# Layer 0 of a four-layer graph kernel: features by twos, bf16 parts moved into the dense sums, loads on other queues

## The chip, the cores and the metric

One Trainium2 chip, one core used. The metric is device time of one execution in microseconds (us), the median over runs. Engines: PE is TensorE (PEld its weight loads), DVE is VectorE, ACT is ScalarE, POOL is GpSimd, SP is SyncE, which only issues transfers here. PEclk is the granted TensorE clock, 1.00 being full speed.

## The reference, cut to what matters

Four layers follow each other on a graph of 4096 nodes with 256 features. Only layer 0, a dense graph attention with 8 heads, is touched by the change:

```python
def _L0_gnn_ref(x, W, b, a, adj_matrix):              # N=4096, D=256, H=8
    node_feats = (x @ W.T + b).reshape(num_nodes, num_heads, half)
    logit_parent = (node_feats * a[None, :, :half]).sum(axis=-1)
    logit_child = (node_feats * a[None, :, half:]).sum(axis=-1)
    attn_logits = logit_parent[:, None, :] + logit_child[None, :, :]
    attn_logits = jax.nn.leaky_relu(attn_logits, 0.2)
    attn_logits = jnp.where(jnp.abs(adj_matrix)[..., None] != 0.0, attn_logits, 0.0)
    attn_probs = jax.nn.softmax(attn_logits, axis=1)
    out = jnp.einsum('ijh,jhc->ihc', attn_probs, node_feats)
    return out.reshape(num_nodes, -1)
# x = layernorm(x + _L0_gnn_ref(...)); three more layers with the same adjacency follow
```

## The kernel before: the parts that matter

Layer 0 has three steps. **Features**, in 32 blocks of 128 nodes: the node features, exponentials of the child logits, their split into a coarse and a fine part (`src`, hi and lo) for the dense sums, and into three bf16 parts (`gb`, stored to `gmd`) for the attention. **Dense sums**: for each of 16 pairs of blocks, the adjacency is loaded (`a`), cast to the matmul's format (`ar`), stored again for the later layers (`adjs`), turned into a bf16 mask (`nad`), and multiplied by `src` into `pz`: 4096 matmuls in 128 groups of 32, one group for each `ar`. **Attention**: in two halves of four heads, signs of logits are compared with the mask and multiplied by the bf16 parts.

```python
# attention: loads, all but `na` on ACT's queue
for half in range(2):
    for b in range(0, NB, 8):
        nc.scalar.dma_start(gm[:, b:b + 8], gmd[half, :, b:b + 8])
    for it in range(N // IT):
        for g in range(NB // K):
            nc.sync.dma_start(na[:, g * K:(g + 1) * K], nad[it, :, g * K:(g + 1) * K, :])
        for hh in range(H // 2):
            nc.scalar.dma_start(lpb, ...)             # parent logits of this head
            nc.scalar.dma_start(z, ...)
            # ... per group of 4 blocks: ACT sg = sign(lpb + lc), DVE gt = sg > na, PE acc += gt^T gm
# ...
# sums0: features, one block at a time, with everything of the block in the loop
work = tile_pool(name="l0aw", bufs=2)
ps   = tile_pool(name="l0aps", bufs=1, space=PSUM)
psz  = tile_pool(name="l0apz", bufs=3, space=PSUM)
for b in range(NB):
    # ... load x, 2 transposes, 2 matmuls -> pn, add the bias -> nf, lp, lc; ex = exp(lc), exp(0.2 lc)
    v = work.tile([P, H, 2, C1], F32, name="v")
    for s in range(2):
        nc.vector.tensor_mul(v[:, :, s, :], nf, ex[:, s]...)
    for i, t in ((0, v[:, :, 1, :]), (1, nf)):        # hi and lo parts for the dense sums
        nc.scalar.copy(hi, t)
        nc.vector.tensor_sub(lo, t, hi)
    gb = work.tile([P, H, 3, 2 * C1], BF16, name="gb")
    nc.scalar.copy(gb[:, :, 0, :], vv)                # three bf16 parts for the attention
    nc.vector.tensor_sub(vv, vv, gb[:, :, 0, :])
    nc.scalar.copy(gb[:, :, 1, :], vv)
    nc.gpsimd.tensor_sub(vv, vv, gb[:, :, 1, :])
    nc.gpsimd.tensor_copy(gb[:, :, 2, :], vv)
    for half in range(2):
        nc.scalar.dma_start(gmd[half, :, b], gb[...])
# ... total = sums of src over all nodes: 64 matmuls, one copy
# dense sums
for b in range(0, NB, 2):
    pz = [psz.tile([P, 2, 512], F32, name="pz") for _ in range(2)]
    for g in range(NB // 4):
        a = work.tile([P, 2, G, P], F32, name="a", bufs=2)
        for q in range(2):
            nc.sync.dma_start(a[:, q], self.adjt[b + q, :, g * G:(g + 1) * G, :])
        ar = work.tile([P, 2, G, P], F32R, name="ar")          # two buffers, from the pool
        nc.vector.tensor_copy(ar, a)
        nb = work.tile([P, G, 2, P], BF16, name="nb")
        for q in range(2):
            nc.scalar.activation(nb[:, :, q, :], a[:, q], AF.Copy, scale=-1.0, bias=1.0)
            nc.gpsimd.dma_start(self.adjs[b + q, ...], ar[:, q])
        nc.gpsimd.dma_start(nad[it, ...], nb)
        # ... 32 matmuls pz[q][:, t] += ar[:, q, k]^T src[:, jc, t, s]
    for q in range(2):
        # ... zt from pz on ACT and DVE, stored to zd
```

## Time and profile before

| | before |
|---|---|
| time, median of 4 runs (lowest to highest) | 5450.6 us (5443.5 to 5451.7) |
| features, until `total` is copied | 224.5 us |
| last dense matmul | 705.5 us |
| first attention matmul, last attention matmul | 734.5, 1710.9 us |
| layers 1 to 3 begin their first large product (`ps_sup`) | 1776.9 us |

The places in time are read from the timeline.

The timeline at the turn between the halves (start, duration, engine; in brackets the idle time before it and what ended it):

```profile
1211.16 0.33 ACTq L216 DMA_DIRECT2D gm<-gmd  x1
...
1216.67 0.59 ACTq L225 DMA_DIRECT2D lpb<-lpd  x1
...
1221.23 4.41 ACTq L225 DMA_DIRECT2D lpb<-lpd  x1
1228.21 8.42 ACT L242 ACTIVATE sg<-lpb,lc 128x1024 bf16<-128x1024 f32 x8 [25.10 <-DMA lpb<-lpd]
```

The last load of `gm` could only go at 1211.16, when half 0 had released its tile; the loads of `lpb` stand behind it in ACT's order, and ACT then waited 25.10 us for them.

### The profile page before, as it was taken

The numbers are of one execution on the slowest core, as the hardware profiler recorded it, in microseconds if no ns is written. First come the engines' busy times: TensorE is split into PE (matmuls) and PEld (weight loads), VectorE is DVE, ScalarE is ACT, GpSimd is POOL, SyncE is SP. The second block draws the span as 40 slices with busy tenths as digits, with TensorE's granted clock in tenths as the row PEclk, the third lists the DMA queues.
The fourth block names the chain that finished last, engine by engine and source line by source line (L and its number), as shares of the span: only waits on it lengthen the run. The fifth ranks groups of instructions, "written<-read, shape, count | busy, mean of one in ns | idle before, by whom it ended". The sixth has DMA issues, their size and how long they took to land. (4 is left out here: it accounts for less than half of the span.)

```text
span 5447.4 us, 72422 instructions
## 1 busy us (share of the span) xinstructions
PE 4418.2 (81%) x25835; PEld 3512.0 (64%) x25836; DVE 3488.5 (64%) x8177; ACT 2870.9 (53%) x5723; POOL 444.1 (8%) x807
## 2 busy tenths in 40 slices
PE   6899967767774899688888888886788888887799
PEld 4699967766774785466666566644555555555677
DVE  4322258887887222877776677619988888888322
ACT  4433369979994103655555555446555555555211
POOL 3344400000001210000000000000000000000000
PEclk6799989999997998799999999997999999999899
DMA  4599953342222593111122211241111111111466
GB/s 150 193 342 346 341 195 106 132 150 91 96 94 74 169 308 104 43 63 63 64 72 72 65 63 63 70 145 37 59 57 57 57 57 57 57 57 59 157 227 202
DMA packets 333884, 655.57 MB, mean 120 GB/s; under 512 B 73537, under 2 KB 146113, under 8 KB 324289
## 3 DMA queue, kind: packets, MB, share of 16 engines
q1 hardware_dynamic: 189824, 436.29, 24.1%
q10 hardware_dynamic: 112960, 113.79, 6.3%
q0 software_dynamic: 30720, 100.69, 4.8%
q8 instruction: 208, 3.41, 0.3%
q14 instruction: 172, 1.40, 0.1%
HBM read 490.46 MB, written 160.17 MB: 119 GB/s over the span
## 5 line engine op out<-in xcount | busy, mean ns | idle before, releaser
L1061 PE MATMUL ps_a<-X,aT 128*128 128x256 f32 x4096 | 1075.0, 421 | 469.5 <-ACT aT L1058 469.5
L1061 PEld LDWEIGHTS ps_a<-X,aT 128*128 128x128 f32 x4096 | 844.8, 212 | 691.2 <-ACT aT L1058 564.0
L249 PE MATMUL acc<-gm,gt 128*128 128x198 bf16 x8192 | 748.3, 250 | 253.0 <-DVE gt L244 241.5
L242 ACT ACTIVATE sg<-lpb,lc 128x1024 bf16<-128x1024 f32 x832 | 870.9, 1135 | 119.5 <-DVE gt L244 78.9
L249 PEld LDWEIGHTS <-gt 128*128 128x128 bf16 x8192 | 694.7, 98 | 306.5 <-DVE gt L244 283.7
L1058 ACT COPY aT<-ps_tp 128x512 f32<-128x512 f32 x512 | 278.9, 583 | 698.3 <-PE ps_tp L1056 698.1
L380 PE MATMUL pz<-src,ar 128*128 128x264 f32 x4096 | 549.7, 294 | 44.9 <-ACT src L337 33.0
L244 DVE TENSOR_TENSOR gt<-sg,na 128x4096 bf16<-128x4096 bf16 x208 | 474.1, 2286 | 164.6 <-ACT sg L242 164.6
L380 PEld LDWEIGHTS pz<-src,ar 128*128 128x128 f32 x4096 | 522.9, 194 | 66.2 <-ACT src L337 43.8
L138 PE MATMUL ps_r<-XD,adj_piece 128*128 128x512 f32 x2048 | 506.2, 399 | 13.0 <-DMA adj_piece<-adjs 7.3
L811 ACT ACTIVATE ja<-e,nc 128x2048 bf16<-128x2048 f32 x256 | 509.6, 1991 | 0.0
L138 PE MATMUL ps_adj<-XD,adj_piece 128*128 128x512 f32 x2048 | 494.9, 399 | 16.3 <-DMA adj_piece<-adjs 11.2
L138 PEld LDWEIGHTS ps_r<-XD,adj_piece 128*128 128x128 f32 x2048 | 376.8, 188 | 152.5 <-DMA adj_piece<-adjs 23.6
L138 PEld LDWEIGHTS ps_adj<-XD,adj_piece 128*128 128x128 f32 x2048 | 385.3, 190 | 100.5 <-DVE XD L113 11.9
L841 DVE SCALAR_TENSOR_TENSOR v<-e,c 128x4096 bf16<-128x4096 f32 x96 | 429.4, 4472 | 1.1
L947 DVE SCALAR_TENSOR_TENSOR e<-e,edge 128x256 f32<-128x256 f32 x1024 | 415.1, 479 | 2.0
L76 POOL TENSOR_SCALAR ln_var<-ln_mv 128x1 f32<-128x1 f32 (+1 forms) x144 | 35.3, 245 | 4522.9 <-DVE ln_mv L74 1680.1
L753 PE MATMUL ps_logit<-kT,q 64*128 64x512 f32 x1024 | 350.8, 654 | 47.6 <-ACT e L757 45.9
L901 DVE MAX8 cand<-v 128x8 f32<-128x256 f32 x1024 | 350.4, 412 | 4.0
L372 ACT ACTIVATE nb<-a 128x512 bf16<-128x512 f32 x256 | 158.2, 629 | 341.6 <-DMA a<-in_adjt_dram 254.7
L757 ACT ACTIVATE e<-ps_logit 128x1024 f32<-128x1024 f32 x256 | 261.8, 1030 | 114.0 <-PE ps_logit L753 110.7
L897 DVE SCALAR_TENSOR_TENSOR v<-e,hi 128x2048 f32<-128x2048 f32 x128 | 300.9, 2351 | 2.1
(281 smaller groups left out, 4798.0 us busy)
## 6 DMA issues: line engine op xcount, KB each, us to landing
adj_piece<-adjs SPq DMA_DIRECT2D x256, 512.0 KB, 5.4
adj_piece<-adjs SPq DMA_DIRECT2D x512, 256.0 KB, 3.5
a<-in_adjt_dram SPq DMA_DIRECT2D x256, 256.0 KB, 5.6
adjs<-ar POOLq DMA_DIRECT2D x256, 256.0 KB, 5.6
na<-nad SPq DMA_DIRECT2D x64, 1024.0 KB, 6.2
nad<-nb POOLq DMA_DIRECT2D x128, 256.0 KB, 5.1
lpb<-lpd ACTq DMA_DIRECT2D x32, 512.0 KB, 5.0
gmd<-gb ACTq DMA_DIRECT2D x64, 198.0 KB, 2.1
```

Source lines behind the costliest of these rows:

```text
L138: nc.tensor.matmul(ps, a[:, k, :], rhs(jc).rearrange("p s d -> p (s d)"), start=(jc == 0), stop=(jc == self.NB - 1))
L242: nc.scalar.activation(sg[:, k, :], lpb, AF.Sign, bias=lc[:, jc, h:h + 1])
L244: nc.vector.tensor_tensor(*flat, ALU.is_gt)
L249: nc.tensor.matmul(acc[:, q, :6 * C1], gt[:, k, q * P:(q + 1) * P], gm[:, jc, hh, :], start=(jc == 0 and q % 2 == 0), stop=(jc == NB - 1 a ...
L380: nc.tensor.matmul(pz[q][:, t, :W], ar[:, q, k, :], src[:, jc, t, s], start=(jc == 0 and s == 0), stop=(jc == NB - 1 and s == 1))
L753: nc.tensor.matmul(pl[:, s, :], q[s * A:(s + 1) * A, :], kT[s * A:(s + 1) * A, c * 512:(c + 1) * 512], start=True, stop=True)
L811: nc.scalar.activation(ja, e[:, s * HALF:(s + 1) * HALF], f, bias=nc1, accum_out=fs[:, i + s:i + s + 1])
L841: nc.vector.scalar_tensor_tensor(junk, e, c, e, op0=ALU.is_ge, op1=ALU.mult, accum_out=S)
L897: nc.vector.scalar_tensor_tensor(v, ec, hi, ec, op0=ALU.is_lt, op1=ALU.mult, accum_out=sb[:, s:s + 1])
L901: nc.vector.max(cand[:, 8 * j:8 * j + 8], v[:, k * 256:(k + 1) * 256])
L947: nc.vector.scalar_tensor_tensor(ec, ec, edge[:, j:j + 1], ec, op0=ALU.is_ge, op1=ALU.mult)
L1061: nc.tensor.matmul(pa[:, :D], aT[:, k * P:(k + 1) * P], X[:, jc, :], start=(jc == 0), stop=(jc == NB - 1))
```

## The change

Its intent: shorten the features (two blocks a step, PSUM buffers of their own, without the bf16 parts), make the bf16 parts beside the dense sums of the first pairs, let the dense sums have two pairs of `pz` buffers, and take the attention's loads off ACT's queue. The diff, cut to its core:

```diff
-            psz = ctx.enter_context(tc.tile_pool(name="l0apz", bufs=3, space=PSUM))
-            for b in range(NB):
-                x = work.tile([P, 1, D], F32, name="x", bufs=3)
+            for b in range(0, NB, 2):
+                x = work.tile([P, 2, D], F32, name="x", bufs=3)
+                px = ps.tile([P, 512], F32, name="ps_x", bufs=2)
+                pn = ps.tile([P, 2, 512], F32, name="ps_nf", bufs=2)
   ... (the same operations, two blocks wide; one subtraction moves from DVE to POOL)
+                for q in range(2):        # the sums for `total`, now inside the loop
+                    for k in range(2):
+                        nc.tensor.matmul(pt[:, :W], one, src[:, b + q, 1, k], ...)
-                gb = work.tile([P, H, 3, 2 * C1], BF16, name="gb")      # no longer here
-                ...
+            pre.close()                   # PSUM of the features is given back
+            nc.scalar.activation(elc, both[:, :, 1, :], AF.Exp)
+            psz = ctx.enter_context(tc.tile_pool(name="l0apz", bufs=4, space=PSUM))
+            def factored(b):
+                v = work.tile([P, H, 2, C1], F32, name="vf")
+                nc.vector.tensor_add(v[:, :, 1, :], part(0, 0), part(0, 1))   # hi + lo again
+                nc.vector.tensor_add(v[:, :, 0, :], part(1, 0), part(1, 1))
+                nc.vector.tensor_mul(v[:, :, 0, :], v[:, :, 0, :], elc[:, b]...)
+                gb = work.tile([P, H, 3, 2 * C1], BF16, name="gb")
+                nc.scalar.copy(gb[:, :, 0, :], v)
+                nc.vector.tensor_sub(v, v, gb[:, :, 0, :])
+                nc.scalar.copy(gb[:, :, 1, :], v)
+                nc.gpsimd.tensor_sub(v, v, gb[:, :, 1, :])
+                nc.gpsimd.tensor_copy(gb[:, :, 2, :], v)
+                for half in range(2):
+                    nc.scalar.dma_start(gmd[half, :, b], gb[...])
             for b in range(0, NB, 2):
                 pz = [psz.tile([P, 2, 512], F32, name="pz") for _ in range(2)]
+                for q in range(2):
+                    factored(b + q)
   ... attention
-                for b in range(0, NB, 8):
-                    nc.scalar.dma_start(gm[:, b:b + 8], gmd[half, :, b:b + 8])
                     for g in range(NB // K):
                         nc.sync.dma_start(na[...], nad[...])
+                        if it == 0:
+                            nc.sync.dma_start(gm[:, g * K:(g + 1) * K], gmd[half, :, g * K:(g + 1) * K])
-                        nc.scalar.dma_start(lpb, ...)
+                        nc.gpsimd.dma_start(lpb, ...)
-                        nc.scalar.dma_start(z, ...)
+                        nc.gpsimd.dma_start(z, ...)
```

## The prediction

> **What bounds the kernel now.** The change touches layer 0 only, so I cut the span there into stages at places read from the timeline: features 0 to 225 us (with the first pair of dense sums between them), dense sums to 706, first loads of the attention to 735, attention half 0 to 1211, the turn between the halves to 1235, half 1 to 1717, and the rest, in which order and forms of the instructions stay as they are. Stretches of the trace, with busy us of each engine, TensorE clock, DMA share, GB/s:
> ```profile
> core 0: us, PE busy (x) PEld busy (x) DVE busy (x) ACT busy (x) POOL busy (x), PEclk, DMA share, GB/s
> 0.00:225.00 225.00, 154.68 (x558) 109.13 (x560) 109.92 (x281) 103.54 (x314) 80.36 (x132) 0.70 0.42 140
> 225.00:706.00 481.00, 468.93 (x3828) 464.27 (x3826) 102.27 (x181) 153.23 (x266) 222.08 (x355) 1.00 0.96 340
> 706.00:735.00 29.00, 1.17 (x7) 0.85 (x8) 7.25 (x20) 8.24 (x9) 0.00 (x0) 0.57 0.85 346
> 735.00:1211.00 476.00, 373.04 (x4095) 346.62 (x4092) 410.57 (x334) 428.31 (x410) 0.00 (x0) 0.99 0.33 117
> 1211.00:1235.00 24.00, 0.27 (x4) 0.14 (x3) 7.15 (x10) 6.79 (x7) 0.00 (x0) 0.59 0.73 271
> 1235.00:1717.00 482.00, 374.46 (x4096) 347.48 (x4094) 415.15 (x343) 428.61 (x410) 0.00 (x0) 0.98 0.25 82
> ```
> In the features no engine is full, the clock is 0.70 and DMA idles more than half the time: a chain from engine to engine. In the dense sums PE is 97% busy at full clock and the DMA share is 0.96: two limits close together. Two stretches, 29 and 24 us, have hardly any PE work. The waits of the first 900 us say why:
> ```profile
> ACT nb L372 <- DMA a<-in_adjt_dram: 254.7, 159, 4.9
> DVE ar L369 <- DMA adjs<-ar: 192.1, 60, 5.7
> ...
> POOL v L345 <- ACT gb L344: 96.1, 32, 4.0
> ...
> DVE nf L317 <- PE ps_nf L314: 64.2, 32, 3.4
> ...
> ACT sg L242 <- DMA gm<-gmd: 15.1, 1, 15.1
> ```
> POOL and DVE wait on ACT and PE once in each of 32 feature blocks: one block's chain hardly overlaps the next. The dense sums wait for DMA on the feeding engines, not on PE: its matmuls waited for `ar` 1.1 us in all. The last line is the gap at 706; at the turn between the halves the same query shows
> ```profile
> PE acc L249 <- DVE gt L244: 94.7, 69, 23.7
> ...
> ACT sg L242 <- DMA lpb<-lpd: 25.1, 1, 25.1
> ```
> and the timeline shows the loads of `lpb` issued at 1216.67 and 1221.23 on ACT's queue, behind the four loads of `gm`, the last of which waited for the end of half 0 (the last matmul of it near 1211).
>
> **What the Trainium skill says.** (1) "TensorE: Matmul & The Clock Gate", section "Part 1: The HAM clock gate": the array runs at half clock unless it has been busy for about 3.4 us. The trace agrees: 0.70 in the features, 1.00 in the dense sums, 0.57 in the gaps. (2) "PSUM — Partial Sum Buffer", section "Specifications (TRN2)": eight banks of 2 KiB per partition. Four `pz` buffers of two banks are thus all of PSUM, and no dense sum can start before the features have closed theirs. The trace of before, with three `pz` buffers, does overlap them. (3) "DMA: Bandwidth & Descriptors", section "Issuing engines are not separate DMA queues": issuing from other engines only saves sequencer time, "usually small relative to the DMA itself". Here it was not small: the load behind `gm` held ACT 25.1 us. (4) "Perfetto Trace Analysis", section "Roofline": 358 GB/s is a core's share of HBM, one core alone can reach about 120% of it. Here the dense sums move 340 GB/s at a share of 0.96, and loads of `na` and `gm` alone some 410.
>
> **The change part by part.**
> *Features by twos.* Before, 32 blocks take about (225 - 12 - 8 for the 64 matmuls of `total`) = 205 us, 6.4 us each, and contain the 256 dense matmuls of pair 0. After, 16 steps of two blocks; nothing of the bf16 parts (ACT 2 x 0.63, DVE 0.71, POOL 1.12 + 0.68 us a block) and no `pz` matmul is in them. PE's work in a step, from pitches in the timeline at low clock (feature matmuls 0.50 us: four in 2.02; the rest estimated from their width): 4 transposes x 0.22 + 4 feature matmuls x 0.50 + 2 small transposes x 0.22 + 4 sums x 0.23 = 4.2 us; at full clock (four in 1.24) about 2.3. The order on PE takes two steps together: features of A and B, then sums of A, sums of B. The sums wait for the longest path, DVE add 0.8, ACT copy 0.63, POOL subtraction 1.12, each with a hop of about 0.1 us. Followed through two steps at low clock I get about 9.7 us, at full clock about 7; I take 8.5. So 8 x 8.5 = 68 us, plus 12 us of start, plus tail and `total`: about 84 us, in place of 225.
> *Dense sums.* PE now has all 4096 matmuls here. Its best pitch before is 85 in 10 us, 0.1176 us, its mean 481/3828 = 0.1257, with dips where one pair's `pz` is read; four buffers remove these. PE alone would need 4096 x 0.1176 = 482 us. But the bytes: `a` 67.1 + `adjs` 67.1 + `nad` 33.5 + `zd` 8.65 + `gmd` 12.7 = 189 MB, of which some 4 MB go early, since only two `a` and two `ar` buffers can fill during the features. At 340/0.96 = 354 GB/s when full, 185 MB take 523 us; at the mean rate of before, 544. I choose 532: DMA becomes the bound, PE has slack. The bf16 parts (per block DVE three adds or multiplications at about 0.45 and 0.71, ACT 1.26, POOL 1.8 us) come some eight per nine groups in the first four pairs, by the order of instructions. There POOL has 1.08 + 0.76 + 1.8 = 3.6 us per group of 32 matmuls, which PE could do in 3.8. So POOL also runs nearly full for the first 36 groups and may make them 5 us each: 36 x 5 + 92 x 3.9 = 539, close to the DMA figure and not to be added to it.
> Features and dense sums end at 84 + 532 = 616, against 706: **-90 us**. Most of what the features gain goes back, since before they carried about 31 MB, some 90 us worth of transfer, under their idle time.
> *First attention loads.* `sg` needs `lpb`, which now goes out on POOL's queue, not what stood behind `gm`. Its first record can come about when `fac` is done, near 713 instead of 727.8. Then four `sg` 4.3 us and `gt` 2.3 us bring the first matmul to about 721 instead of 734.5; `na` and `gm` come in turn, 1.84 MB per group or 4.5 us at 410 GB/s against 4.2 us for four `sg`, so about 1 us is lost again: **-12 us**.
> *The turn between the halves.* `gm` is loaded piece by piece behind `na` on SP as the last head releases it, `lpb` is on another queue and prefetched a head ahead: the 23.7 us wait of PE goes, **-24 us**. In the rest of the attention ACT and DVE are both at 86 to 90% and take turns; two fewer issues per head on ACT were hidden anyway: 0.
> Sum: -90 - 12 - 24 = -126, 5450 - 126 = **5324**.
>
> **Rivals.** (a) PE stays the bound of the dense sums, because the DMA share near 1 counts waiting packets and not capacity. For it: 10 us pieces at 377 GB/s occur; PE hardly waited for `ar`. Against: in twelve such pieces after 235 us the share was 0.90 to 1.01, and the mix is fixed. Then the stage takes about 500 us, the whole 5290. (b) The loop of two `ar` buffers gets longer: cast 0.7, hop, issue 1.1, landing 5.6 make 8.3 us for two groups, 4.15 each, already what PE's mean pace of 4.0 is. POOL is in order, so bf16 work that waits for ACT holds up the writes of `adjs`; with 5.5 us for 36 groups and 4.1 after it the stage takes 575, the whole 5367. The 192 us wait of DVE for `adjs` speaks for it. (c) Two steps do not overlap, since the sums that are now inside the loop wait for POOL: 8 us a step, 16 x 8 = 128 us, end at 144, the whole 5384. Against it: `px` and `pn` have two buffers each, and the work per step is half of before. (d) SWDGE descriptors for `lpb` are slow while DVE works, and the turn keeps a gap: plus 10 to 25 us. Prefetch by a head of 30 us speaks against.
>
> **Range and chances.** The dense stage gives -30 to +40 us, the features -10 to +40, the attention -5 to +15. These do not all go the same way; I take 5270 to 5380. The 2% line is 5341, only 17 us above the centre. I give 0.65 to faster by over 2%, 0.34 to within 2%, 0.01 to slower.
>
> **What would show it right or wrong.** Features: last sum of `total` before about 95 us, clock there not under 0.65, no `pz` matmul earlier. Dense sums: 500 to 560 us long, DMA share at or above 0.97 and near 350 GB/s, PE with visible waits on `ar` in place of waits on `pz`; first four pairs slower than the rest. Attention: no ACT wait on `lpb` or `gm` over 5 us, first matmul about 14 us after the last dense sum, no gap of PE at the turn. After the attention every stage equal to within 5 us. Wrong it is if the dense stage runs at PE's pitch (sum too small), or over 570 us, or if POOL's in-order queue holds PE for more than 30 us in all.

## More of the kernel before

From the page, the span in 40 slices of 136 us (layer 0 is the first thirteen), then the group of the dense matmuls (busy us, mean ns, idle time before them):

```profile
PE   6899967767774899688888888886788888887799
...
PEclk6799989999997998799999999997999999999899
DMA  4599953342222593111122211241111111111466
...
L380 PE MATMUL pz<-src,ar 128*128 128x264 f32 x4096 | 549.7, 294 | 44.9 <-ACT src L337 33.0
```

The first slice and a half are the features: in the first slice PE is at 6, the clock at 6 and DMA at 4. Slices 3 to 5 are the dense sums, where PE and DMA are both near 9. The dense matmuls' idle time is due to `src`, that is to pair 0, which ran inside the features.

## The result, and the profile after

The changed kernel takes 5366.6 us (5364.5 to 5370.0, 4 runs) against 5450.6 us. The ratio is 0.9849, interval 0.9832 to 0.9866: 1.5% faster, and within the 2% band. Ratios and intervals here are from runs of both kernels in the same rounds; they are close to the ratio of the medians quoted, but not quite the same.

The page after, the same rows as above:

```profile
PE   7799977777774997888888888877788888887799
...
PEclk9999999999997997999999999988999999999899
DMA  5899952232223780111112222141111111111466
...
L402 PE MATMUL pz<-src,ar 128*128 128x264 f32 x4096 | 521.3, 289 | 51.7 <-DVE ar L391 51.0
```

The clock is 0.9 from the first slice, and the dense matmuls now wait for `ar` (51.0 us) where they had waited for `src`. In the second slice PE stands at 7 only, though all of it lies in the dense sums. The stretches of time after, cut at its own stages (length, busy us of each engine with its instructions, clock, DMA share, GB/s):

```profile
0.00:88.00 88.00, 58.37 (x289) 43.86 (x290) 46.67 (x105) 41.32 (x94) 28.94 (x47) 0.98 0.34 105
88.00:300.00 212.00, 171.17 (x1277) 167.10 (x1278) 94.97 (x176) 83.05 (x145) 129.01 (x178) 0.92 0.87 303
300.00:660.00 360.00, 349.62 (x2820) 345.22 (x2820) 75.36 (x133) 113.59 (x197) 164.08 (x263) 1.00 0.95 337
660.00:678.00 18.00, 1.67 (x9) 1.04 (x8) 7.77 (x20) 10.04 (x11) 2.89 (x4) 0.56 0.77 271
678.00:1155.00 477.00, 371.83 (x4058) 344.03 (x4057) 407.19 (x333) 431.70 (x413) 24.43 (x33) 0.98 0.35 126
1155.00:1634.00 479.00, 375.86 (x4136) 348.82 (x4133) 418.44 (x347) 430.44 (x412) 25.35 (x34) 0.99 0.27 96
```

The features end at 88 us, at a clock of 0.98. The dense sums take two stretches. In the first, 212 us long, the bf16 parts are made: 1277 matmuls are 39.9 groups of 32, so 5.3 us a group. In the second, 2820 matmuls in 360 us are 88 groups of 4.09 us. The gap before the attention has shrunk from 29 to 18 us, and the row of 24 us at the turn between the halves has gone: the halves meet at 1155 and each lasts as long as before. Stage by stage, from the timeline:

| us | before | after | difference | predicted |
|---|---|---|---|---|
| features, until `total` | 224.5 | 87.4 | | 84 |
| last dense matmul | 705.5 | 660.0 | -45.5 | -90 |
| from there to the first attention matmul | 29.0 | 17.6 | -11.4 | -12 |
| attention, first to last matmul | 976.4 | 956.3 | -20.1 | -24 |
| from there to `ps_sup` | 66.0 | 65.8 | -0.2 | 0 |
| all after it | | | -7.5 | 0 |
| span of the profiled execution | 5447.4 | 5362.7 | -84.7 | -126 |

So the features came as predicted, and so did the two gaps. What is missing is in the dense sums: from 87.8 to 660.0 they took 572 us, not 532. The -7.5 us after `ps_sup` lie in layers whose instructions are the same. They are no more than the scatter of the kernel before over chips (5443.5 to 5456.4 us), and nothing here explains them.

The chain of waits of the kernel after in its first 900 us (engine and tile, what it waited for, total us, times, longest):

```profile
ACT nb L394 <- DMA a<-in_adjt_dram: 233.5, 136, 5.3
...
DVE ar L391 <- DMA adjs<-ar: 134.6, 46, 7.6
...
PE pz L402 <- DVE ar L391: 51.0, 33, 8.6
...
ACT gb L372 <- DMA gmd<-gb: 39.0, 15, 5.8
```

DVE waits 134.6 us for `adjs` stores to release one of the two `ar` buffers, almost all of it (119.9 us) after 300 us. ACT waits for stores of `gmd` to release one of the two `gb` buffers, all of it before 300 us. PE waits for `ar` 40.8 us of its 51.0 between 90 and 290 us. What such a moment looks like in the timeline:

```profile
181.69 0.71 DVE L373 TENSOR_TENSOR vf<-vf,gb 128x528 f32<-128x528 f32 x1 [3.25 <-ACT gb L372]
186.99 0.63 ACT L372 CAST gb<-vf 128x528 bf16<-128x528 f32 x1 [5.33 <-DMA gmd<-gb]
...
187.65 0.71 DVE L373 TENSOR_TENSOR vf<-vf,gb 128x528 f32<-128x528 f32 x1 [5.25 <-ACT gb L372]
...
188.28 1.62 DVE L391 CAST ar<-a 128x1024 fp32r<-128x1024 f32 x1
...
189.95 1.47 PE L402 MATMUL pz<-src,ar 128*128 128x264 f32 x5 [7.28 <-DVE ar L391]
```

ACT stands 5.33 us for a `gmd` store to land. DVE's subtraction stands behind ACT, the cast of `ar` stands behind the subtraction in DVE's order, and PE idles 7.28 us for want of `ar`. What the clock does meanwhile, by the microsecond (busy us of PE, PEld, DVE, ACT and POOL with their instructions, then clock, DMA share, GB/s):

```profile
186.00:187.00 1.00, 0.00 (x0) 0.00 (x0) 0.00 (x0) 0.01 (x1) 0.00 (x0) 1.00 0.17 65
188.00:189.00 1.00, 0.00 (x0) 0.00 (x0) 1.00 (x2) 1.00 (x3) 0.77 (x1) 0.50 0.00 0
191.00:192.00 1.00, 1.00 (x6) 1.00 (x6) 1.00 (x2) 0.00 (x0) 1.00 (x3) 0.50 0.87 156
195.00:196.00 1.00, 1.00 (x10) 1.00 (x9) 0.48 (x2) 0.76 (x2) 0.68 (x2) 1.00 1.14 366
```

PE's last matmul before the wait ends near 182.7. The clock is still 1.00 in the microsecond from 186, then falls to 0.50, and is back at 1.00 in the microsecond from 195, some 5 us after PE has gone on at 189.95. A microsecond holds 6 matmuls at 0.50 and 10 at 1.00.

### The profile page after: what moved, and what is told of

It reads as the page before. It is cut to its first block, busy times and chain, and to the rows that moved or that the text cites. A ratio compares the mean times of both kernels' runs of the same rounds, so it can differ in the third digit from the quotient of the medians.

```text
span 5362.7 us, 72171 instructions
## 1 busy us (share of the span) xinstructions
PE 4366.6 (81%) x25835; PEld 3492.6 (65%) x25836; DVE 3492.0 (65%) x8129; ACT 2851.5 (53%) x5579; POOL 516.3 (10%) x879
## 5 line engine op out<-in xcount | busy, mean ns | idle before, releaser
L243 ACT ACTIVATE sg<-lpb,both 128x1024 bf16<-128x1024 f32 x832 | 871.0, 1135 | 86.7 <-DVE gt L245 86.0
L402 PE MATMUL pz<-src,ar 128*128 128x264 f32 x4096 | 521.3, 289 | 51.7 <-DVE ar L391 51.0
```

The source lines that it names most:

```text
L243: nc.scalar.activation(sg[:, k, :], lpb, AF.Sign, bias=lc[:, jc, h:h + 1])
L402: nc.tensor.matmul(pz[q][:, t, :W], ar[:, q, k, :], src[:, jc, t, s], start=(jc == 0 and s == 0), stop=(jc == NB - 1 and s == 1))
```

## The experiments

The theories going in. **The loop of two `ar` buffers** (the prediction's rival b): an `ar` is free again only when its stores to `adjs` have landed, so two buffers give two groups per round trip. **DMA bytes**: share 0.95 is the limit. For the first stretch: **POOL** is too slow with its part of the bf16 work, **`gb`** buffers come free too late, **DVE's subtraction** holds up the casts, or again **bytes**. Each kernel is the changed one with the edit shown, unless it says otherwise; "ratio" is to the kernel before on the same chip, and "stage" is from the first to the last dense matmul in the profile (572 us in the changed kernel).

### e1: four `gb` buffers

```diff
-                gb = work.tile([P, H, 3, 2 * C1], BF16, name="gb")
+                gb = work.tile([P, H, 3, 2 * C1], BF16, name="gb", bufs=4)
```
(`x` goes from 3 buffers to 2 to make room.)

> The changed kernel with four buffers for the bf16 parts (gb) instead of two (and two for x instead of three, to make room). In the changed kernel the dense sums took 572 us (87.8 to 660.1), where I had put 532; PE waited 40.8 us for ar there between 90 and 290 us, in pockets of some 8 us, one per pair, while ACT waited 39 us in all for the landing of gmd. Theory 1 (pocket: the reuse of gb waits for its own store, in ACT's order, and stands before the casts to nb and, through DVE's order, before the cast to ar): the wait of ACT for gmd falls to under 10 us, the pockets go, the dense stage is 535 to 550 us, the whole 25 to 35 us less than the changed kernel, about 5335. Theory 2 (DMA is full in that stretch with the extra 12.7 MB): the wait moves to another place, stage 565 to 572, the whole within 8 us of 5366. Theory 3 (POOL's order: subtraction and cast between the issues of adjs): stage 560 to 572.

Measured: 5355.8 us, ratio 0.9827 (0.9811 to 0.9844); stage 560.3 us, 12 less, where theory 1 had put 535 to 550. ACT's wait for `gmd` is gone (39.0 to 0). The stretches:

```profile
89.00:300.00 211.00, 180.20 (x1354) 175.57 (x1355) 114.55 (x182) 87.05 (x152) 135.81 (x185) 0.94 0.92 320
300.00:649.40 349.40, 338.84 (x2744) 333.85 (x2743) 72.05 (x127) 110.51 (x191) 160.69 (x255) 1.00 0.95 337
```

The first stretch does 77 more matmuls, but stays at 0.156 us a matmul and a clock of 0.94; the second has the pace of before the edit (0.127 us a matmul). The `gb` wait was real and worth some 12 us; it is not the whole of the first stretch.

### e2: no bf16 work on POOL

```diff
-                nc.gpsimd.tensor_sub(v, v, gb[:, :, 1, :])
-                nc.gpsimd.tensor_copy(gb[:, :, 2, :], v)
+                nc.vector.tensor_sub(v, v, gb[:, :, 1, :])
+                nc.scalar.copy(gb[:, :, 2, :], v)
```

> The changed kernel with the third bf16 part made on DVE (subtraction) and ACT (cast) instead of POOL, so that in the dense sums POOL only issues DMA. Theory 3 (POOL's order holds up the stores of adjs): the first 40 groups go from 5.3 us to about 4.5 us each, stage 535 to 545, the whole about 5335. Theory 1 (gb's reuse waits for the store): the pockets stay, ACT still waits over 30 us for gmd, stage 560 to 575. Theory 2 (DMA): stage 565 to 572. In either of the last two the whole is within 12 us of 5366; ACT's cast could even add a few us.

Measured: 5374.2 us, ratio 0.9860 (0.9843 to 0.9876); stage 576.3 us.

```profile
87.00:300.00 213.00, 170.80 (x1253) 167.16 (x1254) 104.76 (x207) 100.36 (x176) 68.69 (x112) 0.91 0.84 294
```

POOL's busy time in the stretch halves, from 129 to 69 us, and PE does 1253 matmuls in place of 1277. So POOL's load was not what bound it. The work itself went to DVE and ACT, though, and none of it was taken away.

### e3: the bf16 parts stored twice

```diff
-                for half in range(2):
-                    nc.scalar.dma_start(gmd[half, :, b], gb[...])
+                for half in (0, 1, 2, 3):       # the second pair of stores goes to gmd2, read by no one
+                    to = gmd if half < 2 else gmd2
+                    half = half % 2
+                    nc.scalar.dma_start(to[half, :, b], gb[...])
```

> The changed kernel with the store of the bf16 parts doubled (a second copy to another DRAM tensor that nobody reads), 12.7 MB more in the first stretch of the dense sums; the result stays right. Theory 2 (DMA is the limit of that stretch): 12.7 MB at 303 to 350 GB/s are 36 to 42 us more, the whole about 5405. Theory 1 (latency of gb's store in ACT's order): each pocket also gets longer, since gb is held until four stores have landed, so more than that, 45 to 80 us. Theory 3 (POOL): under 20 us more.

Measured: 5409.2 us, ratio 0.9926 (0.9909 to 0.9942); stage 615.3 us, 43 more. The second copy is 13.0 MB (64 stores of 198 KB, with 1024 bytes to the KB; the texts say 12.7), which thus pass at 302 GB/s, the rate of the stretch (303). This fits bytes; it also fits a loop through `gb`, whose two buffers now wait for four stores. The run alone does not tell these apart.

### e4: the bf16 work spread over all 16 pairs

```diff
-            nc.scalar.activation(elc, both[:, :, 1, :], AF.Exp)
+            zero = wp.tile([P, NB // 2 + 1, 1], F32, name="zero")
+            nc.vector.tensor_scalar_mul(zero[:, 0], total[:, :1], 0.0)
   ... in each pair: its own exponentials, which wait for the pair before through a bias of zero
+                nc.scalar.activation(elc[:, b:b + 2], both[:, b:b + 2, 1, :], AF.Exp, bias=zero[:, b // 2])
   ... and at its end
+                nc.vector.tensor_scalar_mul(zero[:, b // 2 + 1], zt[:, 0, 1, :1], 0.0)
```

> The changed kernel with the bf16 parts forced to two blocks per pair over all 16 pairs (their factor exp(lc) is made pair by pair with a zero bias that comes out of the pair before), in place of some eight per pair in the first four pairs; the result stays right. Theory 1 (pocket when gb is reused before its store has landed): gb is free each time, no pockets, stage 535 to 550, the whole about 5335. Theory 2 (DMA full): 11.8 MB per pair at 350 GB/s make 33.8 us, 16 times 541: also about 540, but then with PE waits for ar spread over all pairs, 30 us or more in all, and a DMA share at 0.97 all through. Theory 3: as theory 1. Rival: the new chain from the end of a pair through DVE and ACT costs 2 to 3 us per pair and eats the gain.

Measured: 5375.4 us, ratio 0.9866 (0.9850 to 0.9883); stage 580.2 us.

```profile
86.50:300.00 213.50, 195.82 (x1504) 193.46 (x1505) 69.31 (x120) 73.35 (x130) 104.00 (x160) 0.95 0.90 312
300.00:667.00 367.00, 333.52 (x2594) 328.75 (x2592) 119.39 (x208) 129.15 (x230) 182.58 (x281) 0.97 0.93 324
```

Before 300 us PE does 227 matmuls more, and after it the pace falls from 4.09 to 4.53 us a group. No wait for `gmd` is left, but PE still waits 50.7 us for `ar`, now spread over the pairs. Spreading the bf16 parts did not make them cheaper; how much of the 8 us that were lost is the edit's own chain from pair to pair, the rival in the text, was not tested.

### e5: no stores of `adjs`

```diff
-                        nc.gpsimd.dma_start(self.adjs[b + q, ...], ar[:, q].bitcast(F32))
   ... and the later layers read the adjacency itself, with a casting load
-            nc.sync.dma_start(a.bitcast(F32), self.adjs[...])
+            nc.gpsimd.dma_start(a, self.adjt[...])
```

> The changed kernel without the 67 MB of stores to adjs in the dense sums; the later layers load the tiles of the input adjt itself, through a casting DMA on POOL's queue in place of SP's. Result right. Four buffers, bf16 parts, orders on DVE, ACT and PE stay. Theory DMA (bytes bind the dense sums, at some 335 GB/s): 118 MB are left, 350 us, so PE's pitch of 0.1176 us binds, 482 us plus start and pockets, dense stage 490 to 520 in place of 572, PE waits for ar mostly gone after the bf16 stretch. Rival (in-order waits of ACT and DVE for gmd and nb bind, not the bytes): stage stays above 550. The later layers may lose some us by the other queue; the stage is read from its own profile, the whole is about 5300 if they lose nothing.

Measured: 5334.6 us, ratio 0.9789 (0.9773 to 0.9806), correct; stage 538 us.

```profile
86.00:282.00 196.00, 173.94 (x1295) 169.13 (x1296) 101.88 (x182) 85.45 (x152) 88.69 (x103) 0.94 0.72 235
282.00:624.00 342.00, 342.00 (x2803) 341.96 (x2802) 71.94 (x128) 110.06 (x191) 64.50 (x86) 1.00 0.66 214
```

This takes away a third of the bytes and the long part of the `ar` loop at once, so it does not tell these two apart; e8 does. In the second stretch PE never idles: 342.00 us busy of 342.00, 0.1220 us a matmul. That is PE's pace when nothing holds it. The first stretch also got faster (0.151 us a matmul in place of 0.166), but it is still slow at a DMA share of only 0.72: there it is not DMA capacity that binds.

### e6: the bf16 parts back in the features' loop

`factored(b)` is called inside the features' loop of two blocks; all else as changed.

```diff
+                nc.scalar.activation(elc[:, two], both[:, two, 1, :], AF.Exp)
+                for q in range(2):
+                    factored(b + q)
```

> The changed kernel with one part undone: the bf16 parts are made and stored in the feature steps again (two blocks a step), not in the dense sums. The feature stage had DMA at a share of 0.34 after its change. Theory DMA (the stage moves its bytes at some 335 GB/s): the dense stage loses 12.7 MB, 38 us, and the pockets, 11 us, and is 515 to 530; the features get longer by ACT's 2.5 us of casts and 1.6 us of issues a step or by DVE's 4.2: from 87 to about 140 to 160 us. The sum is 0 to 20 us better than the changed kernel at best, 5350 to 5370. If the holding back was worth what the change meant it to be, it is slower, 5380 to 5400.

Measured: 5388.8 us, ratio 0.9887 (0.9870 to 0.9903).

```profile
0.00:148.00 148.00, 78.00 (x288) 55.30 (x289) 109.54 (x197) 69.82 (x155) 80.92 (x95) 0.76 0.38 126
148.00:674.00 526.00, 511.81 (x4096) 506.17 (x4096) 123.91 (x218) 169.83 (x295) 253.35 (x392) 0.99 0.94 335
```

The features take 60 us longer, the dense sums 46 us less. Holding the bf16 parts back is thus worth 14 us up to the end of the dense sums and some 22 in the times (5388.8 against 5366.6), not 60; the rest of the 22 lies after the dense sums and was not looked into.

### e7: the kernel before, with the new queues only

```diff
-                for b in range(0, NB, 8):
-                    nc.scalar.dma_start(gm[:, b:b + 8], gmd[half, :, b:b + 8])
+                        if it == 0:
+                            nc.sync.dma_start(gm[:, g * K:(g + 1) * K], gmd[half, :, g * K:(g + 1) * K])
-                        nc.scalar.dma_start(lpb, ...)
+                        nc.gpsimd.dma_start(lpb, ...)
   ... z and yd likewise
```

> The kernel before with only the attention's queues of the change (na and gm in turn on SP, lpb, z and yd on POOL). My prediction gave these parts 12 + 24 us. In the changed kernel the first attention matmul comes 17.6 us after the last dense sum (before 28.7) and the attention takes 956 us from first to last matmul (before 976), so 11 + 20 = 31 us. Theory (the parts add up): the whole 5420, that is 27 to 37 us under before. Rival (part of the attention's gain comes from the other layout of lp and lc or of the loads): under 20.

Measured: 5418.9 us, ratio 0.9940 (0.9923 to 0.9957), that is 33 us less by the ratio and 29 by the medians on this chip (5448.1 before).

```profile
225.00:716.00 491.00, 476.13 (x3856) 470.22 (x3854) 101.68 (x181) 153.02 (x267) 221.90 (x356) 1.00 0.94 333
716.00:733.00 17.00, 0.89 (x3) 0.59 (x3) 7.72 (x20) 9.54 (x10) 2.89 (x4) 0.58 0.75 270
```

The gap before the attention is 17 us in place of 29, and the attention takes 955 us in place of 976. Both gains of the queues are shown by this part alone. Its dense sums ended 10 us later than before's in this one profile (715.6 against 705.5), though nothing of them was edited; no run explains that.

### e8: three `ar` buffers

```diff
-                    ar = work.tile([P, 2, G, P], F32R, name="ar")
+                    ar = work.tile([P, 2, G, P], F32R, name="ar", bufs=3)
```
(Room comes from `x`, 2 buffers in place of 3, and `prod` and `lpT`, 1 in place of 2.)

> The changed kernel with three ar buffers in place of two (x with two, prod and lpT with one buffer to make room). Theory loop (two ar buffers and a store of 5.5 us bind the dense sums): DVE's wait for adjs, 134.6 us, falls by more than half, PE's wait for ar from 51 to under 20 us, the dense stage from 572 to 540 or less. Theory DMA (the bytes bind): another wait takes its place (loads of a), stage 560 to 575, the whole 5355 to 5370.

Measured: 5334.8 us (5333.9 to 5337.7), ratio 0.9787 (0.9770 to 0.9803); stage 552 us.

```profile
81.00:279.00 198.00, 160.63 (x1204) 155.80 (x1205) 94.56 (x175) 80.61 (x140) 121.02 (x167) 0.94 0.88 299
279.00:633.30 354.30, 353.89 (x2894) 353.24 (x2892) 75.22 (x135) 114.92 (x201) 168.61 (x271) 1.00 0.97 352
```

The bytes are the same, and after 279 us they move at 352 GB/s where the changed kernel moved 337. PE is busy 353.89 of 354.30 us at 0.1224 us a matmul, e5's pace. Two lines of its waits between 60 and 720 us:

```profile
DVE ar L391 <- DMA a<-in_adjt_dram: 207.7, 72, 5.5
...
PE pz L402 <- DVE ar L391: 32.4, 22, 6.0
```

DVE's wait of 134.6 us for `adjs` is gone; it now waits for the next `a`, nearly all of it after 279 us, where PE waits only 0.4 us for `ar`. So the share of 0.95 at 337 GB/s was not the limit of the DMA engines: it was what two `ar` buffers let through. The first stretch, at 0.164 us a matmul, is as it was. Features ended at 81.0 us, 7 us earlier than in the changed kernel; the edit's smaller buffers stand in their loop, and how that helps was not looked into. The 20 us of the stage are what bears on `ar`; some 5 of the 32 us in the times are in neither.

### e9: three `ar` and four `gb`

The tiles of the features get pools of their own, given back before the dense sums, so that both fit.

```diff
+            fw = pre.enter_context(tc.tile_pool(name="l0af", bufs=2))       # features: x, xT, nf, lpT, ex, v
+            dw = ctx.enter_context(tc.tile_pool(name="l0ad", bufs=2))       # dense: vf, gb, zt
-                gb = work.tile([P, H, 3, 2 * C1], BF16, name="gb")
+                gb = dw.tile([P, H, 3, 2 * C1], BF16, name="gb", bufs=4)
-                    ar = work.tile([P, 2, G, P], F32R, name="ar")
+                    ar = work.tile([P, 2, G, P], F32R, name="ar", bufs=3)
```

> The changed kernel with three ar buffers and four gb buffers; room for them from giving the tiles that only the features use, and those that only the dense sums use, pools of their own in the same space. Three ar buffers alone took the dense stage from 572 to 552 us and the whole to 5335; four gb buffers alone took 11.6 us off the stage. If the two act on different waits, the stage is 535 to 545 and the whole 5320 to 5328, faster than any so far. Rival: in the stretch with the bf16 parts (some 190 us, 5.3 us per group of 32 matmuls in place of 3.9) DVE's order holds the casts to ar whatever the buffers, and nothing is added: stage 550, the whole 5335.

Measured: 5334.4 us, ratio 0.9787 (0.9771 to 0.9803); stage 545.4 us, 7 less than e8's, but the features ended 8.7 us later (89.7), so nothing is gained over e8. It is also a control for e8: here the features keep three `x` buffers, and against e1, which has four `gb` as well, the third `ar` takes 15 us off the stage.

```profile
89.50:285.00 195.50, 168.05 (x1240) 164.81 (x1241) 109.27 (x179) 80.18 (x141) 125.53 (x170) 0.92 0.90 311
```

### e10: e8, with DVE's subtraction on POOL

```diff
-                nc.vector.tensor_sub(v, v, gb[:, :, 0, :])
+                nc.gpsimd.tensor_sub(v, v, gb[:, :, 0, :])
```

> Three ar buffers, and the first bf16 subtraction moved from DVE to POOL, so that DVE, which casts to ar in order, no longer waits for ACT in the bf16 chain. Theory (DVE's order: the subtraction waits for ACT's cast and the next cast to ar stands behind it): the stretch gets faster than with three ar buffers alone, stage 530 to 545. Rival (POOL, with 2 x 1.12 + 0.69 + 1.84 = 4.8 us of work per group, becomes the bound, and holds the stores of adjs): the stretch stays at 5.3 us a group or gets longer, stage 552 to 565, the whole 5335 to 5350.

Measured: 5338.5 us, ratio 0.9796 (0.9780 to 0.9812); stage 552 us, as e8. Its waits of the first 900 us:

```profile
DVE vf L366 <- POOL gb L376: 87.3, 27, 9.8
...
PE pz L402 <- DVE ar L391: 35.2, 15, 7.1
```

DVE no longer waits at the subtraction for ACT, but waits 87.3 us at the addition that begins the next block, for POOL. PE's wait is the same. The wait was moved along the chain, not removed; where the subtraction runs was not the cause.

### e11: the kernel before, with three `ar` buffers

```diff
-                    ar = work.tile([P, 2, G, P], F32R, name="ar")
+                    ar = work.tile([P, 2, G, P], F32R, name="ar", bufs=3)
```

> The kernel before with three ar buffers and nothing else. If the loop of two ar buffers (cast, store of 5.6 us) already held the dense sums before, PE's mean there goes from 0.1257 us towards the 0.121 us that it keeps up with three buffers in the changed kernel: 3828 x 0.0047 = 18 us less, but without a second pair of pz buffers some 10 us of waits for the reading of pz stay: the stage of 481 us becomes 463 to 472, the whole 5433 to 5442. If PE's own pitch bound it, as I read the profile of before: no change, 5445 to 5455.

Measured: 5434.1 us, ratio 0.9965 (0.9948 to 0.9982), 17 us less by the medians on this chip and 19 by the ratio; the last dense matmul came at 700.4 us in place of 705.5, so only 5 us of it are in the stage that was edited, and the rest was not looked into. Two lines of its waits between 60 and 720 us:

```profile
DVE ar L369 <- DMA a<-in_adjt_dram: 252.6, 79, 5.9
...
PE pz L380 <- DVE zt L387: 8.7, 12, 2.3
```

DVE's wait for `adjs`, 192.1 us in the kernel before, is gone here too, but PE had waited only 1.1 us for `ar` there. So a third `ar` alone is worth little to the kernel before: the two buffers kept DVE waiting, and hardly PE. Its dense stretch (0.1257 us a matmul) was already nearer to PE's pace than the changed one's (0.1277).

### e12: one pair of `pz` buffers

```diff
-            psz = ctx.enter_context(tc.tile_pool(name="l0apz", bufs=4, space=PSUM))
+            psz = ctx.enter_context(tc.tile_pool(name="l0apz", bufs=2, space=PSUM))
```

> The changed kernel with one pair of pz buffers (two in place of four): the part two buffer pairs undone. In the changed kernel PE waited 51 us for ar and not for pz. If ar and DMA bind the dense sums, a wait for the reading of pz mostly takes the place of one for ar: stage 572 to 582, the whole 5366 to 5376. If the two pairs were worth what I put for them (PE's mean to its best pitch, 2 us per pair): 30 us more, 5395.

Measured: 5361.8 us, ratio 0.9833 (0.9817 to 0.9849), no slower than the changed kernel; stage 567.5 us. Its waits of the first 900 us:

```profile
PE pz L402 <- DVE zt L409: 32.3, 19, 5.0
PE pz L402 <- DVE ar L391: 10.2, 8, 1.9
```

PE now waits 32.3 us for its PSUM to be read, and 10.2 us for `ar` where it had waited 51.0. One wait took the other's place: while PE stands for `zt`, the next `ar` buffers fill. The second buffer pair was worth nothing here, where `ar` is what PE runs short of.

## Why the prediction was partly right

The range held the result and the class with the higher chance did not come. The result lies 42 us above the centre, about what the prediction had allowed the dense stage on the high side (+40). The lower end, 5270, has no working behind it: the margins, all added on the low side, reach 5279. By the prediction's own steps:

1. **Features by twos: right, in part by luck.** "About 84 us" against 87.4. The step pace also holds: 16 copies of `xT` from 12.5 to 77.1 us are 4.3 us a step, 8.6 for two, against the 8.5 taken. But the 8.5 was taken between 9.7 at low clock and 7 at full clock. The clock came out at 0.98, for which the working gives 7, and 72 us in all; the chain was longer than it was followed, and the two errors nearly cancelled.
2. **First attention loads and the turn: right.** -11.4 and -20.1 us against -12 and -24; e7 shows both from the queues alone. The dread of slow POOL-issued loads (rival d) did not come about: ACT waited 0.4 us for `lpb` in all. One reading was off: before, at the first gap, the load of `lpb` was issued at 708.87, ahead of `gm` (from 712.23). What went out after `gm` was the load of `z`, at 727.37, and the first `sg` came 0.4 us after it.
3. **"I choose 532: DMA becomes the bound, PE has slack": this step failed.** The dense sums took 572 us, and these 40 us are nearly all of the 42 us by which the sum missed (84 gained in the medians, 126 predicted); the smaller misses, +3, +4 and -7.5 us, about cancel. The prediction's own sign of being wrong, a dense stage of over 570 us, came true. Three parts of the step did not hold:
   - *The rate.* 340 GB/s at a share of 0.96 was taken as the DMA engines' limit. e8 moves the same mix at 352 GB/s, so it was not; a piece of 10 us at 377 GB/s stood in the trace of before, and was named under rival (a). In the second stretch of the changed kernel two `ar` buffers set the pace: DVE waited 119.9 us there for `adjs` stores, at 4.09 us a group against the 4.15 that rival (b) worked out from the round trip. With three buffers PE itself is the limit, at 0.1224 us. In the kernel before, the same loop hardly reached PE (e11).
   - *The stretch with the bf16 parts.* The prediction priced it (36 groups of 5 us, then 92 of 3.9, "539 ... not to be added" to the DMA figure) and then did not use it. It was 40 groups of 5.3 us and 88 of 4.09: 212 + 360 = 572. With its own paces the first 40 groups (36 of 5 us and 4 of 3.9) and the other 88 would be 196 + 343 = 539, so the first stretch missed by 16 us and the second by 17. DMA limits and waits in one stage were compared over the whole stage, and the larger taken; but the slow stretch moves its bytes at 303 GB/s, and what it does not move is left for later.
   - *The half clock.* The stretch lost 212 - 1277 x 0.122 = 56 us against full pace. PE's waits for `ar` are some 41 of them; the other 15 are about what the clock takes (8% of 212 are 17 us). The prediction knew of the clock in the features and the gaps, and did not price it for waits in the dense sums. The Trainium skill, "TensorE: Matmul & The Clock Gate", section "HAM oscillation — how this bites in real kernels", describes just this: matmul bursts with waits of 3 to 5 us for data between them restart at half clock each time. The trace agrees: waits up to 8.6 us, a mean clock of 0.92, and a clock of 0.50 for some 4.5 us after the wait of 7.28 us above.
4. **PE's best pitch, 0.1176 us, was too short.** It came from counting 85 matmuls in 10 us, which counts those that overlap the edges too: each lasts 0.28 us, so the pitch is nearer (10 + 0.28) / 85 = 0.121. Where PE never idles, in e5 and e8, it is 0.1220 and 0.1224. PE alone would need 4096 x 0.122 = 500 us, not 482. The floor was nearer to the DMA figure than it seemed.
5. **"Four buffers remove these" dips: right, but worth nothing here.** PE's waits for the reading of `pz` did go (10.6 us before, none after), but e12, with two buffers and 32.3 us of such waits, is no slower.
6. **Rival (b) came closest**, with 575 us for the stage and 5367 for the whole. Its first half, the loop of two `ar` buffers, is shown by e8. Its second half, that POOL's order makes the first stretch slow, was not borne out: without bf16 work on POOL the stretch is no faster (e2), so that its 5.5 us a group came near the measured 5.3 for a reason that is not shown. The Trainium skill, "Perfetto Trace Analysis", section "Optimization Strategy", says that a gap which repeats on the engine that should be full can mean too few buffers for the next tile. The trace agrees for the second stretch: PE's waits for `ar` after 300 us, 10.1 us in 14 times, fall to 0.4 us with a third buffer (e8). The prediction had a line for the loop in hand, 192.1 us of DVE waiting for `adjs`, and its main working read it as DMA being full; but that was DVE, and PE, the engine that should be full, showed no such gap before (1.1 us).
7. Rival (a), PE as the bound, is what the second stretch turns into when a third `ar` is given. It was not reached by the change itself.

**What binds the first stretch stays open.** It runs at 0.151 to 0.170 us a matmul, against 0.122, in all versions that make the bf16 parts beside the first pairs (with e3, which stores them twice, left out). It is no faster without POOL's share of the work (e2) or with a third `ar` (e8), little faster with DVE's subtraction moved (e10, 0.159), and DMA bytes are it only in part (e5: share 0.72, still 0.151). Release of `gb` is some 12 us of it (e1). But e2 and e10 moved work to another engine of the same chain and took none away, and they changed more than its place: between 90 and 280 us DVE's cast of `ar` takes 836 ns in the mean in the changed kernel, 691 in e2 and 1062 in e10 (815 in e8). It was the longer, the more of the bf16 work POOL did beside it; what that costs the stretch was not tested. What is left is only argued: each block's bf16 parts go ACT, DVE, ACT, POOL, each engine takes its work in order, and the casts of `ar` and the masks stand between; any wait in the chain holds up the next `ar`, and the half clock then adds to it. e10 fits this, as its wait moved to the next link; no run takes the chain away while leaving the work. Done inside the features the work cost 60 us there (e6), and beside the dense sums 46.

The experiments also gave a better version than both: e8, 5334.8 us against 5366.6 and 5450.6, 2.1% faster than the kernel before, with an interval (2.0 to 2.3%) that just crosses the 2% line, so whether it is faster by 2% is unclear.

## What to carry to other kernels

A DMA share near 1 and a wait for stores can both come from a loop of too few buffers: before calling DMA the bound, work out the round trip of one buffer (cast, issue, landing) over the number of buffers, and compare it with the pace of the stage. Then look whether the engine that should be full waits at the end of that loop: in the kernel before it hardly did, and a third buffer gained little. Work that is moved out of an idle stage into a full one is not hidden there: price the stretch where it lands by itself, add the clock lost after each wait, and then add the stretches instead of taking the larger of two limits over the whole stage. Where transfers stand behind one that waits for a buffer, another issuing queue can remove the wait: here it was the surest part of the change (e7).

## What the Trainium skill lacked or had wrong

- "DMA: Bandwidth & Descriptors", section "Issuing engines are not separate DMA queues", says that issuing from several engines saves only sequencer time, usually small. It lacks the case where an issue itself waits for a buffer and holds up what stands behind it on its engine: at the turn ACT waited 25.1 us for a load of `lpb` that stood behind the load of `gm`, and moving the queues alone gave about 30 us (e7).
- No page that was read says that a DMA share near 1 can come from the kernel's own loop of buffers: 337 GB/s at a share of 0.95 with two `ar` buffers became 352 GB/s at 0.97 with three, with PE then busy 353.89 of 354.30 us. The point belongs to "Perfetto Trace Analysis", section "Identifying the Most-Contended Engine", which does call the busy share of the DMA engines misleading, but does not name this cause.
